# Layer 0's norms of pairs 2 to 4 applied to the rows as they lie, their mean and scale spread by DMA

## The chip, the cores and the metric

The kernel runs on one core of a Trainium2 chip. The metric is the device time of one launch in microseconds (us), the median of several runs. The engines are named as the profile names them: PE does matmuls and transposes, DVE is the vector engine, ACT the scalar engine, POOL is GpSimd, and SP issues most of the DMAs. Each engine works through its own queue in order.

## The reference

The input x is 8 batches of 512 tokens by 512 features. It passes through two blocks, and each adds its result to x.

```python
x = x + xcond(layernorm(x))   # 4 layers of a gated recurrence, in two directions, and a fusion
x = x + ffn(layernorm(x))     # ternary weights, 512 -> 2048 -> 512, gelu and a layernorm between

def stack(x):                 # once along the tokens, once against them, with the same weights
    h = x
    for i in range(4):
        z = sigmoid(h @ Wz[i].T + bz[i])
        a = clip(1 - z, 1e-8, 1 - 1e-8)
        g = tanh(h @ Wz[i].T + bz[i])          # the same matrix and bias serve both gates here
        h_new = scan(a, z * g)                 # s[t] = a[t] * s[t-1] + (z * g)[t]
        if i > 0:
            h_new = h_new + h
        h = layernorm(h_new) * gamma + beta    # over the 512 features of a token
    return h
```

The two directions' results are joined and multiplied by the fusion matrix. What matters here is the layernorm after layer 0: each token has a mean and a variance over its 512 features.

## The kernel before

**Layout.** The recurrence runs along the tokens, so the states lie with features on the partitions and tokens along the row: a state is four chunks of 128 features by 512 tokens. A layernorm wants the other layout. `norm` therefore does it in two moves. A *turn* (`turned`, `tokens`) takes one tile of 128 tokens: four PE transposes (L316) into the PSUM tile `pt`, of which there are two buffers; then on DVE `bn_stats` (L171), `bn_aggr` (L173), the variance with its epsilon (L177) and the negative mean (L182); on POOL the power -0.5 (L178); on ACT the normalise step (L188, L189) into a token tile. When all four token tiles stand, a *turn-back* (`back`) takes one chunk of features: four PE transposes (L325) into the PSUM tile `pf`, and on ACT the step with gamma and beta (L331) into the state `h`.

**Batches and pairs.** Batches are worked in pairs, (0,1), (2,3), (4,5), (6,7). A sequence `s` is (batch, direction). For one pair, layers 1 to 3 run over its four sequences in turn; each sequence of a layer is four steps of `gates`: eight matmul instructions (L487) for one chunk, three gate functions on ACT (L505 to L507), the clamp on POOL (L511), and on DVE the product (L514), the scan (L518) and the residual (L588). Then `fusion` of this pair (L622, L632; eight tiles of 128 tokens) is interleaved with `first_layer` of the next pair (L535). In layer 0 both directions share the matmul and the gates, and the two scans leave four chunks `zf` (forward) and four chunks `zb` (backward). Layer 0 works on raw x: its product is multiplied by the token's scale `scale[b]` (L546), which `scale_x` makes from four PE transposes of a column spread over 128 columns and one ACT copy (L385, L389).

**The order.** Everything is put in order by hand in `slot`. A slot does its main work, then what is due (`stages`, by name), then a share of the queues `turns` and `backs`, then the slot's scans, then the ACT steps of those shares; `now` counts slots. An entry of a queue is taken in order and only when it is ready: a turn from the slot that it was queued for, a turn-back one slot after its fourth token tile. A slot takes `cap` entries of each queue (2 beside a fusion tile, otherwise 1), and a second one if that entry is late by its `piece`. `pair` sets how many entries share one piece. `held` counts the token tiles in use (a pool of 10), `zlive` the chunks of z (a pool of 16). `need(s)` empties the queues of s before its next layer.

After layer 3, `norm_last` needs only each token's scale, not the mean; for sequences (3,0), (5,0) and (7,0) `by_scalar` measures it on ACT, in two passes with accumulation (`two_passes`, L396 to L398), and for all others DVE does it. During the changes of pairs, each fusion tile also takes up to three `pieces` of another job: weights of the second block are staged by DMA (L646), made ternary on DVE (L193, L194) and stored again (L679).

**The second block** starts when the recurrence is done and isn't touched.

Of the kernel before, what the change touches and what calls it, by code (L numbers as in the profile page):

```python
# [9 lines left out]
F32 = mybir.dt.float32  # L10
F32R = mybir.dt.float32r
AF = mybir.ActivationFunctionType
ALU = mybir.AluOpType
# [3 lines left out]
P = 128  # L17
LN_EPS = 1e-5
# [6 lines left out]
def kernel(  # L25
# [26 lines left out]
    nc = tc.nc  # L52
    B, S, H = x.shape
    L = gru_wT.shape[0]
    F = fc_wT.shape[1]
    NC_ = H // P
    NT = S // P
# [7 lines left out]
    small = ctx.enter_context(tc.tile_pool(name="small", bufs=8))  # L65
    wpool = ctx.enter_context(tc.tile_pool(name="wts", bufs=1))
    hp = ctx.enter_context(tc.tile_pool(name="h", bufs=6))
    dram = ctx.enter_context(tc.tile_pool(name="x1", bufs=1, space=bass.MemoryType.DRAM))

    tokp = ctx.enter_context(tc.tile_pool(name="tok", bufs=TOK))  # L70
    xsp = ctx.enter_context(tc.tile_pool(name="xs", bufs=12))
    zp = ctx.enter_context(tc.tile_pool(name="z", bufs=ZT))
    ps_f = ctx.enter_context(tc.tile_pool(name="ps_f", bufs=2, space=PSUM))
# [34 lines left out]
    gam = const.tile([P, NC_], F32, name="gam")  # L108
    bet = const.tile([P, NC_], F32, name="bet")
# [11 lines left out]
    for i in range(2):  # L121
# [3 lines left out]
        s = fusp.tile([P, P], F32R, name=f"fpick{i}")  # L125
# [36 lines left out]
    ident = const.tile([P, P], F32, name="ident")  # L162
    make_identity(nc, ident)
    mhalf = const.tile([P, 1], F32, name="mhalf")
# [64 lines left out]
    with rec:  # L229
        gp = rec.enter_context(tc.tile_pool(name="gate", bufs=3))  # L230
# [6 lines left out]
        now = [0]  # L237
        state = {}
        rsv = {}
        turns, backs = [], []  # L240

        held = [0]

        class Tokens(list):
# [4 lines left out]
            def append(self, tile_):  # L249
                super().append(tile_)  # L250
                self.at = now[0] + self.lag

        def ready(at):
            if isinstance(at, Tokens):
                return len(at) == NT and at.at <= now[0]
            return at <= now[0] and held[0] < TOK

        def shares(cap):


            last = []
            for q in (turns, backs):
                some = []
                for i in range(max(2, cap)):
                    if not q or not ready(q[0][0]):
                        break
                    at, piece = q[0][:2]
                    late = (at.at if isinstance(at, Tokens) else at) + piece <= now[0]
                    if i >= cap and not late:
                        break  # L270
                    some.append(take(q))
                last = some + last
            return last

        zlive = [0]
# [3 lines left out]
        def queue(q, key, at, piece, go):  # L279
            left[key] = left.get(key, 0) + 1  # L280
            q.append((at, piece, key, go))
# [27 lines left out]
        def turned(zs, t, name, frees=0):  # L309
            def source():  # L310
                if t == NT - 1:
                    zlive[0] -= frees
                spare = name.startswith("00_0") and t > 1
                pt = (ps_f if spare else ps_t).tile([P, H], F32, tag="pf" if spare else "pt", name=f"pt_{name}")
                for c in range(NC_):
                    nc.tensor.transpose(pt[:, ts(c, P)], zs[c][:, ts(t, P)], ident)  # L316
                return pt
            return source
# [21 lines left out]
        def norm(s, zs, tag, pause, pair=1):  # L340

            toks, at = Tokens(), now[0] + pause

            def dst():
                if s not in state:
                    state[s] = hp.tile([P, NC_, S], F32, tag="h", name=f"h_{s[0]}{s[1]}")
                return state[s]

            for t in range(NT):
                queue(turns, s, at, t // pair, tokens(turned(zs, t, f"{tag}_{t}", NC_), toks, None, f"{tag}_{t}"))  # L350
            for c in range(NC_):
                queue(backs, s, toks, c // pair, back(toks, dst, c, True, f"{tag}_{c}"))

        def norm_last(s, tag):
            rsv[s] = small.tile([P, NT], F32, tag="rsv", name=f"rsv_{tag}")
            zs = [state[s][:, c, :] for c in range(NC_)]
            for t in range(NT):
                source, name = turned(zs, t, f"{tag}_{t}"), f"{tag}_{t}"
                queue(turns, s, now[0] + NC_ + 1, t, by_scalar(s, t, source, name) if s[0] > 1 and s[0] % 2 and s[1] == 0 else
                      tokens(source, None, rsv[s][:, t : t + 1], name))  # L360

        def by_scalar(s, t, source, name):

            def go():
                src = source()
                left[s] += 1

                def last():
                    end = two_passes(src, src, rsv[s][:, t : t + 1], name)

                    def rest():
                        end()
                        left[s] -= 1
                    stages.append((now[0] + 1, "late", rest))
                return last
            return go

        rx, scale = {}, {}

        def scale_x(b):  # L380

            def go():
                pf = ps_f.tile([P, S], F32, tag="pf", name=f"pr_{b}")
                for t in range(NT):
                    nc.tensor.transpose(pf[:, ts(t, P)], rx[b][:, t : t + 1].broadcast_to([P, P]), ident)  # L385

                def last():
                    scale[b] = gp.tile([P, S], F32, tag="scale", bufs=2, name=f"scale_{b}")
                    nc.scalar.copy(scale[b], pf)  # L389
                return last  # L390
            return go
# [56 lines left out]
        stages = []  # L448
# [64 lines left out]
        def product(z, t):  # L513
            nc.vector.tensor_tensor(z, z, t, ALU.mult)  # L514
# [7 lines left out]
        def first_layer(b, lag=0):  # L522


            zf, zb = [], []

            def chunk(o):
                def work():
                    while zlive[0] + 2 > ZT:
                        slot(None, 2)  # L530
                    zlive[0] += 2
                    name = f"{b}_0_{o}"
                    u = ps_u.tile([P, S], F32, tag="u", name=f"u_{name}")
                    for c in range(NC_):
                        nc.tensor.matmul(  # L535
                            u, lhsT=gw[0][:, c, ts(o, P)], rhs=xT[b][:, c, :],
                            start=(c == 0), stop=(c == NC_ - 1),
                        )
                        if (b, o, c) in midway:
                            midway.pop((b, o, c))()  # L540

                    wait = 1 if (b, o) == (0, 0) else 0

                    def scaled():
                        z = zp.tile([P, S], F32, tag="z", name=f"z_{name}")
                        nc.vector.tensor_tensor(z, u, scale[b], ALU.mult)  # L546
                        a, t = factors(z, z, 0, o, name)

                        stages.append((now[0], "clamps", lambda: clamp(nc.gpsimd, a)))
                        if wait:  # L550
                            for i, v in enumerate((bet, gam)):
                                nc.vector.tensor_copy(both[:, :, i, :], v.unsqueeze(2).broadcast_to([P, NC_, 64]))

                        def scans():
                            product(z, t)
                            f = zp.tile([P, S], F32, tag="z", name=f"zf_{name}")
                            scan(f, a, z, False)
                            zf.append(f)
                            if o == NC_ - 1:
                                state[b, 0] = xT.pop(b)  # L560
                                norm((b, 0), zf, f"{b}0_0", 2 if b == 1 else 1, 2 if b < 2 else 1)

                            def backward():
                                scan(z, a, z, True)
                                zb.append(z)
                                if o == NC_ - 1:
                                    norm((b, 1), zb, f"{b}1_0", 2 if b == 1 else 1, 2 if b < 2 else 1)
                            if b == 0:
                                stages.append((now[0] + 1, "resid", backward))
                            else:  # L570
                                backward()
                        stages.append((now[0] + 1 - wait, "scans", scans))
                    stages.append((now[0] + lag + wait, "factors", scaled))
                return work
            return [chunk(o) for o in range(NC_)]
# [295 lines left out]
    for i in range(2):  # L871
# [5 lines left out]
        s = const.tile([P, P], F32R, name=f"pick{i}")  # L877
# [137 lines left out]
    for j in range(ends):  # L1015
        b, k = divmod(j, NF)
        late = []
# [22 lines left out]
        at = 12 if b == 0 else 8  # L1040
# [57 lines left out]
```

## Time and profile before

| | |
|---|---|
| median of 3 runs | 1713.0 us (1712.42 to 1713.18) |
| the profiled execution | 1712.95 us, its span 1711.2 us |
| busy in the span | PE 1700.3, DVE 1389.1, ACT 1089.5, POOL 377.2 us |
| granted TensorE clock | 1.00 throughout |
| recurrent part | the last fusion begins at 1158.9 us |
| changes of pairs | 263.9 to 358, 561.9 to 656, 859.6 to 953 us |

An execution's time is longer than its span by what lies around the first and the last instruction. The page's groups give for each line its engine, the tile written and the tiles read, the shape, the count, the busy time and mean length of one, and the engine's idle time just ahead of it. Matmul lengths overlap one another, so a group's busy time divided by its count is the share of one. Busy times of engines may all be high at once, since they work beside each other; what sets the time is in the chain.

### The profile page before, as it was taken

How to read it: one execution, taken by the hardware profiler on the slowest of the kernel's cores; microseconds unless marked ns; L12 is line 12 of the kernel's file. 1: busy time of each engine (PE TensorE's matmuls, PEld its weight loads, DVE VectorE, ACT ScalarE, POOL GpSimd, SP SyncE). 2: the span in 40 equal slices, each digit the busy share in tenths (PEclk: the TensorE clock that was granted, in tenths of full speed). 3: DMA queues.
4: the chain of work that ended last, by engine and by line, in shares of the span. 5: the costliest groups of instructions: out<-in, count | busy, mean ns of one | idle time of the engine just before them, and what ended most of it. 6: DMA issues, size and time to landing. Idle time of an engine off the chain costs nothing.

```text
span 1711.2 us, 19776 instructions
## 1 busy us (share of the span) xinstructions
PE 1700.3 (99%) x6440; PEld 1042.6 (61%) x6440; DVE 1389.1 (81%) x2619; ACT 1089.5 (64%) x1918; POOL 377.2 (22%) x558
## 2 busy tenths in 40 slices
PE   9999999999999999999999999999999999999999
PEld 5455554555555455555545555554688888888887
DVE  7988889889887888888788888885568768768877
ACT  5898873468886346888535688862356566666654
POOL 3333333223332222333222222321000000000000
PEclk9999999999999999999999999999999999999999
DMA  7002231150000125000012200102201101100100
GB/s 271 19 25 81 98 93 37 66 193 19 13 1 1 56 68 191 19 13 1 1 56 75 98 28 22 75 1 99 74 1 50 50 1 50 50 21 30 50 19 31
DMA packets 46599, 91.75 MB, mean 54 GB/s; under 512 B 5280, under 2 KB 5536, under 8 KB 45472
## 3 DMA queue, kind: packets, MB, share of 16 engines
q1 hardware_dynamic: 45488, 88.78, 15.1%
q10 hardware_dynamic: 1008, 1.70, 0.3%
q8 instruction: 51, 0.84, 0.2%
q14 instruction: 52, 0.43, 0.1%
HBM read 65.30 MB, written 25.17 MB: 53 GB/s over the span
## 4 chain that ended last, share of the span: by engine, by line
PE 92%; DVE 5%; ACT 2%; POOL 1%; issue 0%; DVEq 0%
PE u L487 33%; PE po L937 14%; PE ph L910 14%; PE pu L622 13%; PE u L535 6%; PE pt L316 6%; PE pf L325 4%; DVE z L518 1%; PE py L214 1%; DVE z L514 1%; DVE st L171 1%; ACT tok L189 1%; DVE z L588 1%; PE pst L948 0%; POOL rs L178 0%
## 5 line engine op out<-in xcount | busy, mean ns | idle before, releaser
L487 PE MATMUL u<-xT,gw 128*128 128x512 f32 x768 | 345.5, 593 | 0.0
L487 PE MATMUL u<-h,gw 128*128 128x512 f32 x768 | 345.5, 592 | 0.0
L518 DVE TENSOR_TENSOR_SCAN z<-a,z 128x512 f32<-128x512 f32 x224 | 277.1, 1237 | 21.8 <-DVE z L514 0.9
L511 POOL TENSOR_SCALAR a<-a 128x512 f32<-128x512 f32 x224 | 150.3, 671 | 559.2 <-ACT a L505 558.3
L487 PEld LDWEIGHTS u<-xT,gw 128*128 128x128 f32 x768 | 138.6, 190 | 138.7 <-issue 137.0
L487 PEld LDWEIGHTS u<-h,gw 128*128 128x128 f32 x768 | 138.6, 190 | 138.2 <-issue 138.2
L505 ACT ACTIVATE a<-u,ngb 128x512 f32<-128x512 f32 x192 | 131.7, 686 | 142.4 <-PE u L487 140.9
L937 PE MATMUL po<-pwq,ghi 128*128 128x512 f32 x512 | 202.8, 396 | 0.0
L171 DVE BATCH_NORM_STATS2 st<-pt 128x6 f32<-128x512 f32 x244 | 169.3, 694 | 39.2 <-PE pt L316 32.5
L937 PE MATMUL po<-pwq,glo 128*128 128x512 f32 x512 | 199.7, 390 | 0.0
L910 PE MATMUL ph<-yhi,fcq 128*128 128x512 f32 x512 | 199.7, 390 | 0.0
L910 PE MATMUL ph<-ylo,fcq 128*128 128x512 f32 x512 | 199.4, 389 | 0.0
L514 DVE TENSOR_TENSOR z<-z,t 128x512 f32<-128x512 f32 x224 | 154.8, 691 | 52.6 <-ACT z L507 52.3
L914 ACT ACTIVATE g<-ph 128x512 f32<-128x512 f32 x128 | 76.4, 597 | 186.6 <-PE ph L910 186.6
L178 POOL TENSOR_TENSOR rs<-ve,mhalf 128x1 f32<-128x1 f32 x192 | 125.5, 654 | 155.1 <-DVE nmu L182 152.7
L189 ACT ACTIVATE tok<-pt,nmr,rs 128x512 f32<-128x512 f32 x192 | 149.4, 778 | 6.4
L925 DVE TENSOR_TENSOR acc<-acc,g 128x512 f32<-128x512 f32 x112 | 77.4, 691 | 85.0 <-ACT g L914 84.1
L507 ACT ACTIVATE z<-u,gb 128x512 f32<-128x512 f32 x192 | 132.4, 690 | 0.0
L506 ACT ACTIVATE t<-u,gb 128x512 f32<-128x512 f32 x192 | 130.8, 681 | 0.0
L316 PEld LDWEIGHTS pt<-ident,z 128*128 128x128 f32 x640 | 78.7, 141 | 77.2 <-issue 48.9
L535 PE MATMUL u<-xT,gw 128*128 128x512 f32 x256 | 114.8, 593 | 0.8 <-DVE gw L767 0.8
L622 PE MATMUL pu<-fw,xT 128*128 128x512 f32 x256 | 115.2, 593 | 0.0
(164 smaller groups left out, 2621.0 us busy)
## 6 DMA issues: line engine op xcount, KB each, us to landing
xf<-in_x_dram SPq DMA_DIRECT2D x32, 256.0 KB, 5.5
x<-xf SPq DMA_DIRECT2D x32, 256.0 KB, 2.0
xy<-x SPq DMA_DIRECT2D x32, 256.0 KB, 4.0
xn<-in_x_dram SPq DMA_DIRECT2D x31, 256.0 KB, 4.5
out_dram<-xy SPq DMA_DIRECT2D x31, 256.0 KB, 2.0
xT<-in_xt_dram SPq DMA_DIRECT2D x7, 1024.0 KB, 7.7
fca<-in_fc_wT_dram SPq DMA_DIRECT2D x16, 256.0 KB, 2.9
pwa<-in_proj_wT_dram SPq DMA_DIRECT2D x16, 256.0 KB, 2.6
```

What stands on the lines that cost most here:

```text
L171: nc.vector.bn_stats(st, src)
L189: nc.scalar.activation(dst, src, AF.Identity, bias=nmr, scale=rs)
L316: nc.tensor.transpose(pt[:, ts(c, P)], zs[c][:, ts(t, P)], ident)
L487: nc.tensor.matmul(u, lhsT=gw[l][:, c, ts(o, P)], rhs=h[:, c, :], start=(c == 0), stop=(c == NC_ - 1),)
L507: nc.scalar.activation(z, u, AF.Sigmoid, bias=gb[:, l, o : o + 1])
L511: engine.tensor_scalar(a, a, CLAMP_HI, CLAMP_LO, ALU.min, ALU.max)
L514: nc.vector.tensor_tensor(z, z, t, ALU.mult)
L518: nc.vector.tensor_tensor_scan(dst[:, d], a[:, d], z[:, d], 0.0, ALU.mult, ALU.add)
L535: nc.tensor.matmul(u, lhsT=gw[0][:, c, ts(o, P)], rhs=xT[b][:, c, :], start=(c == 0), stop=(c == NC_ - 1),)
L622: nc.tensor.matmul(pu, lhsT=hs[d][:, c, ts(t, P)], rhs=fw[:, d * NC_ + c, :], start=(c == 0), stop=(c == NC_ - 1),)
L910: nc.tensor.matmul(ph, lhsT=w, rhs=ys[b][c][i], start=(c == 0 and i == 0), stop=(c == NC_ - 1 and i == 1),)
L937: nc.tensor.matmul(po[b][t], lhsT=part[:, ts(t, P)], rhs=pwq[k // NP_][:, k % NP_, :], start=(k == 0 and i == 0), stop=(k == NF - 1 and i ...
```

## The change

For batches 2 to 7, layer 0's two norms no longer turn the tokens back. The chunks `zf` and `zb` stay as they lie. Each token's mean and scale are found from the turned tiles (turns 0 and 1 by ACT in two passes with accumulation, turns 2 and 3 by DVE's `bn_stats`) and gathered in one tile `pk` of 128 x 2 x 4. One POOL instruction makes the four scales. `to_rows` then turns `pk` with one PE transpose, copies the eight rows to SBUF on ACT, stores them as two rows of 512 in DRAM, and loads each row spread over all 128 partitions into a tile of the token pool. `apply` subtracts the one and multiplies by the other on DVE, chunk by chunk, in place; ACT applies gamma and beta as before. Such a chunk is ready three slots after the rows were sent (`LANDS`). Batches 0 and 1 keep the old way.

The token scale of x of batches 2 to 7 goes the same way: one transpose, one ACT copy, a store and one spread load in place of four transposes and a copy. Last, `by_scalar` now also serves (2,0), (4,0) and (6,0), and the norms of layer 0 of batches 3, 5 and 7 are queued in pieces of two.

```diff
+        class Rows:
+            at = None
         def ready(at):
+            if isinstance(at, Rows):
+                return at.at is not None and at.at <= now[0]
...
+        LANDS = 3
+        def to_rows(cols, n, dsts, tag):
+            turned_ = ps_f.tile([P, S], F32, tag="pf", name=f"prow_{tag}")[0 : n * NT, 0:P]
+            nc.tensor.transpose(turned_, cols.rearrange("p i t -> p (i t)"), ident)
+            short = dsts[0][0 : n * NT, 0:P]
+            nc.scalar.copy(short, turned_)
+            row = dram.tile([n, S], F32, tag=f"row_{tag}", name=f"row_{tag}")
+            nc.sync.dma_start(out=row.rearrange("i (t p) -> (i t) p", p=P), in_=short)
+            for i, dst in enumerate(dsts):
+                nc.sync.dma_start(out=dst, in_=row[i : i + 1, :].broadcast_to([P, S]))
+
+        def norm_rows(s, zs, tag, pause, pair=1):
+            rows_, at = Rows(), now[0] + pause
+            pk = small.tile([P, 2, NT], F32, tag="pk", bufs=6, name=f"pk_{tag}")
+            wide = []
+            def close():
+                nc.vector.tensor_scalar(pk[:, 1, :], pk[:, 1, :], LN_EPS, None, ALU.add)
+                nc.gpsimd.tensor_tensor(pk[:, 1, :], pk[:, 1, :], mhalf.broadcast_to([P, NT]), ALU.pow)
+                stages.append((now[0] + 1, "late", send))
+            def send():
+                for i in range(2):
+                    wide.append(tokp.tile([P, S], F32, tag="tok", name=f"wide{i}_{tag}"))
+                to_rows(pk, 2, wide, tag)
+                rows_.at = now[0] + LANDS
+            def turn(t):
+                source, name = turned(zs, t, f"{tag}_{t}"), f"{tag}_{t}"
+                def go():
+                    src = source()
+                    if t == 0:
+                        held[0] += 2
+                    if t >= 2:
+                        st = small.tile([P, 6], F32, tag="st", name=f"st_{name}")
+                        nc.vector.bn_stats(st, src)
+                        nc.vector.bn_aggr(pk[:, :, t], st)
+                        if t == NT - 1:
+                            close()
+                        return lambda: None
+                    def last():
+                        sm, ss = (small.tile([P, 1], F32, tag=k, name=f"{k}_{name}") for k in ("sm", "ss"))
+                        mean, var = pk[:, 0, t : t + 1], pk[:, 1, t : t + 1]
+                        nc.scalar.activation(src, src, AF.Copy, accum_out=sm)
+                        nc.scalar.activation(mean, sm, AF.Copy, scale=1.0 / H)
+                        nc.scalar.activation(src, src, AF.Square, bias=mean, scale=-1.0, accum_out=ss)
+                        nc.scalar.activation(var, ss, AF.Copy, scale=1.0 / H)
+                    return last
+                return go
+            def apply(c):
+                def go():
+                    nc.vector.tensor_tensor(zs[c], zs[c], wide[0], ALU.subtract)
+                    nc.vector.tensor_tensor(zs[c], zs[c], wide[1], ALU.mult)
+                    zlive[0] -= 1
+                    if c == NC_ - 1:
+                        held[0] -= 2
+                    def last():
+                        if s not in state:
+                            state[s] = hp.tile([P, NC_, S], F32, tag="h", name=f"h_{s[0]}{s[1]}")
+                        nc.scalar.activation(
+                            state[s][:, c, :], zs[c], AF.Identity,
+                            bias=bet[:, c : c + 1], scale=gam[:, c : c + 1],
+                        )
+                    return last
+                return go
+            for t in range(NT):
+                queue(turns, s, at, t // pair, turn(t))
+            for c in range(NC_):
+                queue(backs, s, rows_, c // pair, apply(c))
...
-                queue(turns, s, now[0] + NC_ + 1, t, by_scalar(s, t, source, name) if s[0] > 1 and s[0] % 2 and s[1] == 0 else
+                queue(turns, s, now[0] + NC_ + 1, t, by_scalar(s, t, source, name) if s[0] > 1 and s[1] == 0 else
...
+            def spread_x():
+                scale[b] = gp.tile([P, S], F32, tag="scale", bufs=2, name=f"scale_{b}")
+                to_rows(rx[b].unsqueeze(1), 1, [scale[b]], f"x{b}")
+            if b > 1:
+                return spread_x
...
-                                norm((b, 0), zf, f"{b}0_0", 2 if b == 1 else 1, 2 if b < 2 else 1)
+                                (norm if b < 2 else norm_rows)((b, 0), zf, f"{b}0_0", 2 if b == 1 else 1, 2 if b < 2 or b % 2 else 1)
...
-                                    norm((b, 1), zb, f"{b}1_0", 2 if b == 1 else 1, 2 if b < 2 else 1)
+                                    (norm if b < 2 else norm_rows)((b, 1), zb, f"{b}1_0", 2 if b == 1 else 1, 2 if b < 2 or b % 2 else 1)
```

More of the change, by code (lines that the diff above doesn't have):

```diff
@@ L267, in shares @@
                     at, piece = q[0][:2]
-                    late = (at.at if isinstance(at, Tokens) else at) + piece <= now[0]
+                    late = (at.at if isinstance(at, (Tokens, Rows)) else at) + piece <= now[0]
                     if i >= cap and not late:
```

## Prediction, made before the change was run

> **What bounds the kernel now.** I read the page's busy line and slices first, then the chain, then the groups that the change touches, and last the stretches around one change of pairs.
>
> ```profile
> PE 1700.3 (99%) x6440; PEld 1042.6 (61%) x6440; DVE 1389.1 (81%) x2619; ACT 1089.5 (64%) x1918; POOL 377.2 (22%) x558
> ...
> PE   9999999999999999999999999999999999999999
> ...
> DVE  7988889889887888888788888885568768768877
> ...
> PE 92%; DVE 5%; ACT 2%; POOL 1%; issue 0%; DVEq 0%
> ```
>
> PE is never free and holds 92% of the chain: whatever leaves PE shortens the run, as long as no other engine makes PE wait. But DVE stands at 80 to 90% in the recurrent part (slices 1 to 28): it is the next bound, and it has about a tenth to give. These groups carry the edit:
>
> ```profile
> L514 DVE TENSOR_TENSOR z<-z,t 128x512 f32<-128x512 f32 x224 | 154.8, 691 | 52.6 <-ACT z L507 52.3
> ...
> L171 DVE BATCH_NORM_STATS2 st<-pt 128x6 f32<-128x512 f32 x244 | 169.3, 694 | 39.2 <-PE pt L316 32.5
> ...
> L325 PE MATMUL pf<-ident,tok 128*128 128x128 f32 x768 | 112.4, 273 | 1.2 <-ACT tok L189 1.0 <-ACT h L331 0.2
> ```
>
> Now the stretches round the second change of pairs, from batches 2, 3 to 4, 5 (columns: window, length, busy PE, PEld, DVE, ACT, POOL). I number its slots from 0, the first fusion tile; slots 0 to 15 are the fusion tiles and layer-0 chunks, and slot 16 is the first of layer 1.
>
> ```profile
> 580.00:600.00 20.00, 20.00 (x60) 9.70 (x59) 19.24 (x32) 3.62 (x8) 4.16 (x6) 1.00 0.24 79
> 627.20:639.70 12.50, 12.50 (x46) 6.66 (x45) 10.62 (x24) 6.81 (x12) 2.73 (x4) 1.00 0.40 122
> 639.70:655.60 15.90, 15.90 (x54) 8.15 (x53) 12.43 (x19) 4.84 (x7) 0.61 (x1) 1.00 0.52 176
> 655.60:673.50 17.90, 17.51 (x67) 9.43 (x66) 15.63 (x40) 14.73 (x27) 6.58 (x10) 1.00 0.80 277
> 673.50:691.20 17.70, 17.70 (x71) 9.85 (x70) 14.59 (x29) 14.38 (x26) 4.97 (x8) 1.00 0.14 47
> ```
>
> Slots 12 to 23 take 627.2 to 691.2: 64.0 us, PE full but for 0.39, DVE busy 53.3. The first row is the fullest that DVE gets anywhere: 96%.
>
> **PE.** A group of four transposes holds PE 0.4375 us (the chain: "0.87 PE pf L325 x8"), so 0.109 each; the row's mean of 273 ns is overlapped length. Twelve norms (6 batches, 2 directions) lose 16 turn-backs and gain one transpose: 12 x 15 = 180. Six x scales go from 4 transposes to 1: 18. Together 198 x 0.109 = **21.7 us off PE**, of which 6 x 3 x 0.109 = 2.0 are the x scales and 6.6 fall in each of the three changes of pairs. The Trainium skill ("TensorE: Matmul & The Clock Gate", Part 4) gives some 275 ns for a 128x128 transpose inside a kernel. By it the saving would be an estimated 54 us, and the rows' pitch contradicts it.
>
> **DVE, the price.** Each norm gains a subtract and a multiply over four chunks. A dependent pair runs as L514 before a scan does: 0.79 to the dependent start and 0.61 to the next, 1.4 us, so 5.6 a norm. It loses two of four stats (a whole group has a pitch of 1.07: 0.73 + 0.22 + 0.07 + 0.05) to ACT, and in the other two the 0.13 of variance and shift.
>
> When this lands is read from the code. A norm's turns come when its scans are done; the row is sent one slot after the last turn; the chunks are taken from three slots later. So (4,0): turns in slots 8 to 10, sent 11, chunks in 14 and 15. (4,1): turns 10 to 12, sent 13, one chunk in each of 16 to 19. (5,0): turns 15, 16, sent 17, chunks in 20, 21. (5,1): turns 17, 18, sent 19, chunks in 22, 23. All sixteen pairs fall into slots 14 to 23, close before layer 1 reads what they make, and twelve of them into slots whose PE part has just become shorter (an undisturbed gates slot with one turn and one turn-back was 4.31; now 3.44 to 4.42).
>
> DVE in slots 12 to 23: 53.3 + 16 x 1.4 = 75.7, less four whole groups (4.3) and small ones (0.3): 71.1. PE alone would need 64.0 - 0.4 - 6.3 = 57.3. **DVE now has more to do than the stretch lasted.** With DVE never idle it is 71.1 - 64.0 = 7.1 longer, and 0.3 is saved in slot 11: +6.8 a change of pairs, the floor. At 96%, its fullest row, 71.1/0.96 = 74.0: +9.8.
>
> PE cannot run ahead of DVE there: it needs chunk 3 of h(4,1) at slot 20, made in slot 19 behind all of slot 18's scans; h(5,0) at 24 from slot 21; and the turns of layer 1 at 21 need slot 19's residual. The lag of a slot with 6.5 of DVE against 3.9 of PE is passed on, and in the run after it PE is full again, so it isn't won back.
>
> **ACT.** Turns 0 and 1 of each norm are measured by ACT. Two such turns in the profile of before, in ACT's own order of time:
>
> ```profile
> 569.36 0.58 ACT L396 ACTIVATE pt<-pt 128x512 f32<-128x512 f32 x1 [5.90 <-PE pt L316]
> ...
> 570.99 0.59 ACT L396 ACTIVATE pt<-pt 128x512 f32<-128x512 f32 x1
> ```
>
> One takes 1.63, and the new one has a further small copy (L397, 0.20): 1.85. In slots 15 and 17 two stand together, 3.7, behind the affine steps (0.67 each) and ahead of the next slot's three gate functions (1.75). Slot 17 asks 1.75 + 0.2 + 0.67 + 3.7 = 6.3 of ACT against 4.4 of PE. They also hold both pt buffers, so PE's turns of slots 16 and 18 wait for them. I walked the three queues slot by slot with these pitches, on the clock of before. PE unhindered would begin slot 16 at 652.4. DVE makes (4,0)'s last chunk at 656.1, behind three ternary pieces (3.6), ACT its affine step at 656.9 and the two turns until 660.5; so PE's slot 17 begins at 660.9, 4.2 late. ACT's turns of slot 17 end at 672.0, and slot 19 begins 7.0 late; slot 21, behind (4,1)'s last chunk, 8.4. Slots 24 and 25 wait for DVE's stats (slots 21 to 23 hold 6.5 of DVE each) and the tokens behind them, and slot 26 begins at 710.2, against 699.3 in the profile of before: 10.8. The x stats in slot 21 (1.0), the third ternary's load in slot 15 (0.9) and 0.1 at each hand-over bring it to 13.8. I keep that as the upper end, since every queue order in it has to be right, and 9.8 as the value. What ACT loses (four normalise steps at 1.07) lies earlier or beside this.
>
> **POOL.** One power of 128x4 (1.02, L956) takes the place of four (0.65): nothing. But the clamp L511 is 614 ns in the median and 1594 at most, and DVE's L616 took 1.08 and L194 1.04 where they met a clamp, against 0.68 and 0.75. The Trainium skill ("SBUF — State Buffer", SBUF: two separate sides) calls the port pair of the two engines an exclusive lock for a whole instruction when DVE has two SBUF inputs; the new steps have that. By the rows a meeting costs DVE 0.3 to 0.4. Eight of the gates slots hold new steps: 0 to 3.0 a change of pairs; I take 1.5.
>
> **DMA and SP's queue.** Each norm adds a 4 KB store and two spreads of 256 KB; each x scale a store and one spread. By the rows a store lands in 2.0 (x<-xf) and a load in 4.0 to 4.5 (xy, xn): about 7 with the issues. From send to use PE has 15, 18, 11.6 and 10.9 us, so it is covered; uncovered it would be up to 7 each. SP waits at each store for ACT's copy, and behind it stand the staged ternary loads (L646), the stores of x1 (L635) and the loads of xn. The third ternary of slot 15 waited 1.55 for its load already. The others are wanted much later. The x scales were copied at 546.98 and 555.16, and the first fusion tile alone, ahead of the first layer-0 chunk, runs from 561.85: covered by the 6.7 us between and that tile (6.9): nothing.
>
> **Last norm by ACT for even batches.** 12 turns move 1.03 each off DVE onto ACT (1.63), in slots where ACT idles 2.03 before each gate (541 to 562). Nothing, and some 0.3 a turn if that cover were gone.
>
> **Sum.** Per change of pairs: 9.8 + 1.5 = 11.3, PE's saving there already inside. Three of them +33.9, x scales -2.0: +31.9. The profiled execution took 1712.95 (span 1711.2 and 1.75 around it), the median is 1713.0: **1745**. The ends: floor 3 x 6.8 - 2.0 = +18.4, 1731; walk with meetings 3 x 16.8 - 2.0 = +48.4, 1761.
>
> **The rivals.** *PE's saving comes through.* DVE's slack is taken up and PE stays full: 1712.95 - 21.7 = 1691. For it speaks PE's 99%; against it that DVE would have to do 71.1 us of work in 57. It decides if DVE's new steps spread over 71.1/0.96 = 74 us of PE time or more, that is some four slots more than I give them, without PE needing them: 0.09. *A draw.* Part of the lag is hidden by work of the next layer: within 3.4 us of before, 0.04. *The round trip is late too.* In the window of slots 15 to 17 the xf loads took 9.5 to land: with that, (5,0) and (5,1) come up to 2.7 late. As PE waits for the same chunks it adds 2 x 2.7 x 3 = 16: 1761, 0.10. *It doesn't do what it says:* each back queue is served in order, so none of the 16 turn-backs can stay; no weight of its own.
>
> **The numbers.** My forecast holds 0.77. A measurement of this kernel can tell about 0.2%, 3.4 us, from no change. Faster 0.09, same 0.04, slower 0.87. Below 1718 lie the rival of PE, the draw and a little of the slower cases, 0.15; above 1762 some 0.05. The slower cases' own range is 1728 to 1762.
>
> **What would show it.** Right: pf<-ident,tok falls from 768 to 576; new DVE groups of 48 subtracts and 48 multiplies at 0.69; in the 50 us after slot 14 of each change DVE at 95% or more, PE's digit under 9 there, and PE waits for DVE's stats, ACT's passes and h; elsewhere as before. DVE's busy sum rises by 96 x 0.69 - 24 x 0.88 - 48 x 0.3 + 2 - 12 x 0.88, about 22. Wrong: PE at 99% still and slots 14 to 23 no longer than the 51.5 us of before (639.7 to 691.2); or waits of DVE on the spread tiles, which would make DMA the cause.

## The result, and the profile after

The change makes the kernel slower: a median of 1757.4 us against 1712.8, a ratio of 1.0261 (95% interval 1.0243 to 1.0279), 44.6 us more. The forecast was 1745, with a range of 1718 to 1762. The profiled execution took 1758.03, its span 1756.0. One of the four executions of one kernel below (all stats on DVE) took 3579.0 us and is left out of its time.

The page's busy line, the slices of PE, DVE and the granted clock, and the chain by engine:

```profile
PE 1702.9 (97%) x6242; PEld 1025.8 (58%) x6242; DVE 1416.8 (81%) x2559; ACT 1104.8 (63%) x2038; POOL 366.8 (21%) x522
...
PE   9999999988999998799999889999999999999999
...
DVE  8988888889887888898688898876468778768777
...
PEclk9999999989999999999999999999999999999999
...
PE 81%; DVE 13%; ACT 3%; issue 1%; DMA 1%; POOL 1%; DVEq 0%; ACTq 0%
```

PE has 198 transposes fewer, and yet it is busy for longer: 1702.9 us against 1700.3. It also idles 53.1 us of the span (1756.0 - 1702.9) where it idled 10.9. Its digit falls below 9 in three places, the slices after each change of pairs, and nowhere else. DVE has gone from 5% to 13% of the chain.

The groups after (the same columns as before):

```profile
L581 PE MATMUL u<-xT,gw 128*128 128x512 f32 x768 | 363.1, 617 | 8.1 <-ACT xT L429 8.1
...
L332 PE MATMUL pf<-ident,tok 128*128 128x128 f32 x576 | 86.9, 274 | 8.9 <-ACT tok L189 8.7 <-ACT h L338 0.2
...
L421 DVE TENSOR_TENSOR zf<-zf,wide 128x512 f32<-128x512 f32 x24 | 17.5, 728 | 0.8
...
L420 DVE TENSOR_TENSOR z<-z,wide 128x512 f32<-128x512 f32 x24 | 16.4, 682 | 0.0
```

The turn-backs have gone from 768 to 576, as they should. DVE's new steps last 0.68 to 0.73 us in the mean, and DVE never idled ahead of the subtracts (0.0; the forward group's row says the same): the spread rows were always there in time. The recurrence's matmuls over the forward direction's states (they lie in `xT`) hold PE 363.1 us for the same 768 instructions that took 345.5: a slower clock, not more work.

Round the second change of pairs, the stretches of slots 12 to 15, 16 to 19, 20 to 23, and then slots 24, 25 and most of 26 (window, length, busy PE, PEld, DVE, ACT, POOL, granted clock, the DMA engines' busy share, GB/s):

```profile
642.37:667.83 25.46, 25.46 (x72) 11.87 (x71) 23.32 (x35) 7.81 (x16) 2.25 (x3) 1.00 0.55 163
667.83:694.23 26.40, 20.70 (x60) 9.46 (x59) 20.66 (x33) 16.64 (x39) 4.47 (x5) 0.87 0.34 113
694.23:710.96 16.73, 15.54 (x47) 7.10 (x46) 15.48 (x26) 11.02 (x19) 4.75 (x5) 1.00 0.70 251
710.96:735.00 24.04, 15.40 (x43) 7.01 (x42) 21.64 (x41) 14.55 (x26) 7.02 (x9) 0.86 0.13 44
```

Slots 12 to 15 are shorter by what PE lost: 25.46 against 28.41 (627.23 to 655.64). Slots 20 to 23 are 0.94 shorter (16.73 against 17.67). That is all the gain there is in these stretches. Slots 16 to 19 take 26.40 against 17.85, and the last stretch 24.04, not quite to the end of slot 26, against 12.5 for the whole of the same three slots. From the start of slot 12 to the start of slot 26 it is 86.4 (642.37 to 728.75) against 72.1.

What PE waits for there, in PE's order of time:

```profile
672.34 3.48 PE L581 MATMUL u<-xT,gw 128*128 128x512 f32 x4 [2.63 <-ACT xT L429]
...
687.05 0.66 PE L323 MATMUL pt<-ident,z 128*128 128x128 f32 x4 [1.49 <-ACT pt L412]
...
718.07 0.66 PE L323 MATMUL pt<-ident,z 128*128 128x128 f32 x4 [3.52 <-ACT tok L189]
...
724.46 0.55 PE L323 MATMUL pt<-ident,z 128*128 128x128 f32 x3 [2.29 <-ACT tok L189]
...
728.48 0.48 PE L332 MATMUL pf<-ident,tok 128*128 128x128 f32 x1 [2.56 <-ACT tok L189]
```

The first is slot 16 waiting for the affine step of a chunk that DVE made late; the second is slot 18 waiting for a PSUM tile that ACT is still measuring; the last three are slots 24 and 25, where a token tile is late. The releaser named is ACT, but the chain shows who made ACT late. In order of time (start, length):

```profile
705.91 0.61 DVE zf L420
706.54 0.69 DVE zf L421
707.23 0.61 DVE zf L420
707.87 0.69 DVE zf L421
708.56 0.61 DVE st_x L171
...
709.57 0.61 DVE z L608
710.27 1.24 DVE z L612
711.53 0.92 DVE z L682
712.45 0.62 DVE st L171
```

DVE works without a wait through its work of slots 20 to 24: two chunks' steps, x's stats, the product, the scan and the residual, and only then the stats that a waiting turn needs.

### The profile page after: what moved, and what is told of

Read it like the earlier page. It is cut to its first block, busy times and chain, and to the rows that moved or that the text cites. A ratio compares the mean times of both kernels' runs of the same rounds, so it can differ in the third digit from the quotient of the medians.

```text
span 1756.0 us, 19487 instructions
## 1 busy us (share of the span) xinstructions
PE 1702.9 (97%) x6242; PEld 1025.8 (58%) x6242; DVE 1416.8 (81%) x2559; ACT 1104.8 (63%) x2038; POOL 366.8 (21%) x522
## 3 DMA queue, kind: packets, MB, share of 16 engines
q1 hardware_dynamic: 50048, 96.71, 16.3%
## 4 chain that ended last, share of the span: by engine, by line
PE 81%; DVE 13%; ACT 3%; issue 1%; DMA 1%; POOL 1%; DVEq 0%; ACTq 0%
PE u L581 28%; PE po L1031 13%; PE ph L1004 13%; PE pu L716 10%; PE u L629 6%; PE pt L323 5%; PE pf L332 3%; DVE z L612 3%; DVE z L608 2%; DVE z L682 1%; DVE st L171 1%; DVE zf L421 1%; DVE z L421 1%; PE py L214 1%; DVE zf L420 1%
## 5 line engine op out<-in xcount | busy, mean ns | idle before, releaser
L581 PE MATMUL u<-xT,gw 128*128 128x512 f32 x768 | 363.1, 617 | 8.1 <-ACT xT L429 8.1
L581 PEld LDWEIGHTS u<-xT,gw 128*128 128x128 f32 x768 | 144.3, 198 | 157.3 <-issue 142.6
L171 DVE BATCH_NORM_STATS2 st<-pt 128x6 f32<-128x512 f32 x184 | 127.7, 694 | 29.9 <-PE pt L323 22.9
L323 PE MATMUL pt<-ident,z 128*128 128x128 f32 x640 | 96.1, 275 | 22.7 <-ACT tok L189 16.2
L629 PE MATMUL u<-xT,gw 128*128 128x512 f32 x256 | 115.0, 593 | 1.1 <-DVE gw L861 0.8
L716 PE MATMUL pu<-fw,h 128*128 128x512 f32 x256 | 115.1, 592 | 0.0
```

The lines of the kernel that those rows point to most:

```text
L171: nc.vector.bn_stats(st, src)
L581: nc.tensor.matmul(u, lhsT=gw[l][:, c, ts(o, P)], rhs=h[:, c, :], start=(c == 0), stop=(c == NC_ - 1),)
L629: nc.tensor.matmul(u, lhsT=gw[0][:, c, ts(o, P)], rhs=xT[b][:, c, :], start=(c == 0), stop=(c == NC_ - 1),)
L716: nc.tensor.matmul(pu, lhsT=hs[d][:, c, ts(t, P)], rhs=fw[:, d * NC_ + c, :], start=(c == 0), stop=(c == NC_ - 1),)
```

## The experiments

Theory A is that of the prediction: DVE's queue, with ACT's two-pass turns, holds PE in slots 14 to 25. Theory B is the round trip of the rows. A third question came from the profile: what the slower clock costs. Each time stands beside runs of the kernel of before on the same chip, 1712.6 to 1712.7.

**The x scales alone.** The last norms and layer 0's norms are as before.

```diff
-(norm if b < 2 else norm_rows)((b, 0), zf, f"{b}0_0", 2 if b == 1 else 1, 2 if b < 2 or b % 2 else 1)
+norm((b, 0), zf, f"{b}0_0", 2 if b == 1 else 1, 2 if b < 2 else 1)
-(norm if b < 2 else norm_rows)((b, 1), zb, f"{b}1_0", 2 if b == 1 else 1, 2 if b < 2 or b % 2 else 1)
+norm((b, 1), zb, f"{b}1_0", 2 if b == 1 else 1, 2 if b < 2 else 1)
-by_scalar(s, t, source, name) if s[0] > 1 and s[1] == 0 else
+by_scalar(s, t, source, name) if s[0] > 1 and s[0] % 2 and s[1] == 0 else
```

> Only the x scales go through the row and its spread; layer 0's norms and the last norms are as before. Theory A (PE is the bound, and the extra DMAs are covered): 18 transposes of 0.109 us leave PE, 1712.8 - 2.0 = 1710.8, and PE stays full. Theory B (the round trip is waited for): the first layer-0 chunk of a pair waits for its scale, and the time is at or above 1713.

1710.9 against 1712.6, a ratio of 0.9991 (0.9982 to 0.9999). PE's busy time falls from 1700.3 to 1698.0. This small part of the change does about what PE's count says (1.7 us of the 2.0).

**DVE's steps left out.**

```diff
-                    nc.vector.tensor_tensor(zs[c], zs[c], wide[0], ALU.subtract)
-                    nc.vector.tensor_tensor(zs[c], zs[c], wide[1], ALU.mult)
```

> The change without DVE's 96 subtract and multiply steps: the rows are still measured, sent and spread, but not applied, so layer 0's states are left unnormalised. Theory A (DVE's queue, with ACT's two-pass turns, holds PE): DVE has 71.1 - 22.4 = 48.7 us to do in slots 12 to 23 against 57.3 of PE, and PE's saving comes through, less the waits for ACT's turns in slots 16 and 18 (0 to 3 us a change of pairs): 1691 to 1701, granted clock 1.00. If ACT's turns were the main cause, the time would stay above 1730. It doesn't tell the round trip apart, as nothing waits for the rows here.

1696.2, a ratio of 0.9904 (0.9890 to 0.9917). Its busy line:

```profile
PE 1680.8 (99%) x6242; PEld 1020.3 (60%) x6242; DVE 1351.5 (80%) x2463; ACT 1100.5 (65%) x2038; POOL 367.0 (22%) x522
```

The same PE, ACT and DMA instructions as the change, the clock at 1.00, and 61 us faster. So the 96 steps, 65 us of DVE's busy time (1416.8 - 1351.5), cost 61 us of the kernel's. It also parts the change's loss cleanly, span against span: 1756.0 - 1694.0 = 62.0, of which 39.9 are PE's idle time (53.1 - 13.2) and 22.1 are PE's busy time (1702.9 - 1680.8), the same instructions at a lower clock.

**The steps kept, the wait for the rows taken away.**

```diff
-                    nc.vector.tensor_tensor(zs[c], zs[c], wide[0], ALU.subtract)
-                    nc.vector.tensor_tensor(zs[c], zs[c], wide[1], ALU.mult)
+                    nc.vector.tensor_tensor(zs[c], zs[c], scale[s[0]], ALU.subtract)
+                    nc.vector.tensor_tensor(zs[c], zs[c], scale[s[0]], ALU.mult)
```

> The change with both DVE steps of every chunk as they are, but reading the batch's x scale, which has long lain in SBUF, in place of the two spread rows; the rows are still sent and spread, and the normalisation is wrong by that. Theory A (DVE's work): nothing changes, 1757 within 3. Theory B (PE and DVE wait for the round trip): the waits go, and it falls to 1745 or below.

1757.5, a ratio of 1.0263 (1.0249 to 1.0277) where the change has 1.0261. Theory B falls: nothing waits for the trip through DRAM. `LANDS` is still 3 in this run, so the chunks are taken in the same slots; what it costs that the trip puts DVE's steps three slots behind the send was not tested by itself.

**Half the length.** Both steps over the first 256 tokens.

```diff
+                    nc.vector.tensor_tensor(zs[c][:, 0 : S // 2], zs[c][:, 0 : S // 2], wide[0][:, 0 : S // 2], ALU.subtract)
+                    nc.vector.tensor_tensor(zs[c][:, 0 : S // 2], zs[c][:, 0 : S // 2], wide[1][:, 0 : S // 2], ALU.mult)
```

> The change with the subtract and the multiply over the first 256 of 512 tokens only (the other half stays unnormalised). Theory A: DVE's added work falls from 22.4 to about 12 us a change of pairs; its 61 us stand against 57 of PE, so most of the loss goes: 1700 to 1722. If the number of steps or the hand-over counted and not their length, it would stay above 1745.

1733.2, a ratio of 1.0119 (1.0103 to 1.0134): between the two expectations, and so a miss for theory A's number. The half-width steps are more than half as long (lines of the group: duration in ns, least, median and most):

```profile
L420 DVE TENSOR_TENSOR zf<-zf,wide x24: 398/416/419, 346.4 to 999.3; 128x256 f32<-128x256 f32 x24
```

At 0.42 against 0.69 they leave three fifths of the added work, and three fifths of the loss remain (37.0 of 61.3 us above the kernel without them). The loss goes with DVE's added time. My 1700 to 1722 took DVE's sum against PE's sum over the whole stretch, as if one could fill the other's gaps.

**All stats on DVE.**

```diff
-                    if t >= 2:
+                    if t >= 0:
```

> The change with all four turns of each norm measured by DVE's bn_stats, none by ACT. If ACT's two-pass turns (two together in slots 15 and 17) are what carries the walk from 9.8 to 13.8 us a change of pairs, the waits of slots 16 and 18 for pt go and the time falls by up to 12: 1745, less what DVE's 4 more groups in slots 12 to 23 (0.95 each, 3.8) give back, 11 us: 1746 to 1757. If DVE's queue alone is the bound, the 3.8 come on top: 1765 to 1770.

1762.6, a ratio of 1.0292 (1.0275 to 1.0309), 5 us above the change and between the expectations. DVE's 11.4 us more (3 x 3.8) cost only some 5; by this difference ACT's two-pass turns are worth about 6 us, 2 a change of pairs. It is a difference of two terms that I didn't measure apart. In the change itself PE's waits for a tile that ACT is measuring come to 3.1 us in all (three waits for L412), so by both numbers ACT's turns are a small part of the loss.

**The subtract on POOL.**

```diff
-                    nc.vector.tensor_tensor(zs[c], zs[c], wide[0], ALU.subtract)
+                    nc.gpsimd.tensor_tensor(zs[c], zs[c], wide[0], ALU.subtract)
```

> The change with the subtract on POOL and only the multiply on DVE. By DVE's work alone this is like the half-width steps: about 1733. But a two-input step on POOL may be longer than DVE's 0.69, its clamps stand behind it, and the two engines' two-input steps may block one another: if they do, 1745 or above, with longer multiplies or clamps in the groups.

1796.6, a ratio of 1.0484 (1.0467 to 1.0502): 39 us worse than the change. POOL's step and DVE's multiply (ns, least, median, most):

```profile
L420 POOL TENSOR_TENSOR zf<-zf,wide x24: 1262/1358/1713, 342.0 to 1055.5; 128x512 f32<-128x512 f32 x24
```

```profile
L421 DVE TENSOR_TENSOR z<-z,wide x24: 677/692/1736, 370.8 to 1072.9; 128x512 f32<-128x512 f32 x24
```

The step is twice as long on POOL, DVE's multiply must wait for it in DVE's queue (46 us in 24 waits, over both directions), and some multiplies grow to 1.74. The work left DVE, but DVE's queue stood still for it.

**The ternary pieces earlier.**

```diff
-                    pieces((1, 2, 1, 0, 1, 2, 2, 3)[t + (b % 2) * NT])
+                    pieces((3, 2, 2, 1, 1, 1, 1, 1)[t + (b % 2) * NT])
```

> The change with the same twelve ternary pieces a change of pairs taken earlier: 3, 2, 2, 1 beside the first batch's fusion tiles and 1 each beside the second's, so slots 14 and 15 hold two in place of five. Theory A: 3.6 us less of DVE ahead of slot 16 and no wait for a staged load there; slot 16's wait for the last chunk (2.4 to 3.1) and part of ACT's lateness behind it go: 3 to 5 a change of pairs, 1742 to 1748. If only the slots of layer 1 count, no change: 1757.

1743.2, a ratio of 1.0176 (1.0160 to 1.0191): 14 us back, 4.7 a change of pairs. The wait in slot 16 for a chunk is gone; those of slots 18, 24 and 25 stand as they were (1.49, 3.52, 2.29 and 2.56).

**Idle matmuls in PE's gaps.**

```diff
+        def fill(n):
+            if n:
+                dump = ps_u.tile([P, S], F32, tag="u", name=f"dump_{now[0]}")
+                for _ in range(n):
+                    nc.tensor.matmul(dump, lhsT=gw[1][:, 0, 0:P], rhs=gw[1][:, 1, :], start=True, stop=True)
```

> The change with idle matmuls (128x512, 0.86 us each, read by nobody) put into PE's gaps: 3 ahead of slot 16, 2 at the end of slot 18, 4 of slot 24, 2 of slot 25 and 3 ahead of the next turn-back, 42 in all, 36 us of PE. If PE's clock, which reads 0.50 for some us after a wait of 2.3 to 3.5, costs time on the chain, the granted clock returns to 1.00 and the time falls, though PE is given more to do: by 8 to 15, 1742 to 1749. If the slow stretches lie beside DVE's queue and cost nothing, 1757 or above.

1752.9, a ratio of 1.0234 (1.0219 to 1.0250), against 1.0261 for the change: 4.5 us faster with 38.5 us more of PE work (84 instructions). Without the fills PE is busy for 1723.5 - 38.5 = 1685.0, close to the 1680.8 of the kernel without DVE's steps, and the granted clock is 0.998. So nearly all of the slow clock went, and only 4.5 us of the time with it: it lies between what I expected of a clock on the chain (1742 to 1749) and beside it (1757 or more). By that, most of the 22 us of slower matmuls lay beside DVE's queue. The 4.5 is not a clean price of the clock: the two ratios' intervals overlap a little (one ends at 1.0250, the other begins at 1.0243), and the fills may themselves delay a turn here and there, so the clock's share may be larger.

**The last norms of even batches by DVE again.**

```diff
-by_scalar(s, t, source, name) if s[0] > 1 and s[1] == 0 else
+by_scalar(s, t, source, name) if s[0] > 1 and s[0] % 2 and s[1] == 0 else
```

> The change with the last norms of (2,0), (4,0) and (6,0) measured by DVE again, as before. The prediction costed that move at nothing, as ACT idles 2.0 us ahead of each gate there: 1757 within 2. If that move loads ACT where it matters, it is faster by up to 10; if it frees DVE where DVE is short, slower by up to 12.

1757.8, a ratio of 1.0261 (1.0247 to 1.0275). That part of the change costs and gives nothing.

**One norm of four, where DVE has room.** Only the forward norm of batches 2, 4 and 6, two slots after the send, with the pieces earlier and the x scales spread.

```diff
-(norm if b < 2 else norm_rows)((b, 0), zf, f"{b}0_0", 2 if b == 1 else 1, 2 if b < 2 or b % 2 else 1)
+(norm if b < 2 or b % 2 else norm_rows)((b, 0), zf, f"{b}0_0", 2 if b == 1 else 1, 2 if b < 2 else 1)
-(norm if b < 2 else norm_rows)((b, 1), zb, f"{b}1_0", 2 if b == 1 else 1, 2 if b < 2 or b % 2 else 1)
+norm((b, 1), zb, f"{b}1_0", 2 if b == 1 else 1, 2 if b < 2 else 1)
-        LANDS = 3
+        LANDS = 2
-                queue(backs, s, rows_, c // pair, apply(c))
+                queue(backs, s, rows_, c // 2, apply(c))
-                    pieces((1, 2, 1, 0, 1, 2, 2, 3)[t + (b % 2) * NT])
+                    pieces((3, 2, 2, 1, 1, 1, 1, 1)[t + (b % 2) * NT])
```

(The last norms are as in the kernel of before.)

> Only the forward norm of the first batch of each pair (2, 4, 6) goes to the rows, with its chunks two slots after the send, in slots 13 and 14; the other three norms turn back as before; the x scales are spread; the ternary pieces are taken earlier (3, 2, 2, 1 and 1, 1, 1, 1); last norms as before. Theory A: DVE gains 5.6 us a change of pairs in slots that have that much to spare (29 of DVE against 30.5 of PE in slots 12 to 16), so PE's 15 x 0.109 us come through: 1712.6 - 2.0 - 4.9 = 1705.7, 1704 to 1709. If any application on DVE costs more than it saves, it stays above 1711.

**1705.0**, a ratio of 0.9954 (0.9940 to 0.9968): faster than both kernels, and 0.7 from the number worked out. Its busy line:

```profile
PE 1692.9 (99%) x6377; PEld 1035.7 (61%) x6377; DVE 1398.6 (82%) x2610; ACT 1085.8 (64%) x1933; POOL 370.9 (22%) x549
```

PE is busy for 7.4 us less than before (the count gave 6.9), and idles 10.2 of the span of 1703.1 where it idled 10.9. So the gain is work that has left PE. The run changes several things at once; only the pieces (next run) and the x scales (first run) are told apart, `LANDS` 2 is not.

**The same with the pieces where they were.**

```diff
-                    pieces((3, 2, 2, 1, 1, 1, 1, 1)[t + (b % 2) * NT])
+                    pieces((1, 2, 1, 0, 1, 2, 2, 3)[t + (b % 2) * NT])
```

> The same with the ternary pieces where they were (1, 2, 1, 0 and 1, 2, 2, 3). Theory A: slots 12 to 16 then hold 3.6 us more of DVE, about 33 against 30.5 of PE; the pieces of slot 15 no longer stand ahead of a chunk that layer 1 waits for, so 0 to 2 us a change of pairs are lost again: 1705 to 1711.

1723.2, a ratio of 1.0060 (1.0047 to 1.0072): 18 us above the last one and outside what I expected. The work of each engine is the same in both; only the slots of the twelve ternary pieces of a change of pairs differ: eight or four of them beside the first batch's fusion tiles, two or five in slots 14 and 15. The stretch 660 to 670 us of the two, the earlier pieces first (the columns as above):

```profile
660.00:670.00 10.00, 9.84 (x38) 5.31 (x37) 9.27 (x23) 8.81 (x17) 4.71 (x7) 1.00 1.01 366
```

```profile
660.00:670.00 10.00, 5.93 (x19) 3.48 (x18) 8.01 (x19) 6.14 (x11) 2.27 (x4) 0.83 0.62 196
```

And the chain of the second through its gap, in order of time:

```profile
657.34 0.76 DVE pwq L194
658.12 2.49 DMA wq_pw<-pwq
...
661.24 0.75 DVE pwq L194
661.99 0.62 DVE st L171
...
664.00 0.79 ACT tok L189
...
664.83 0.73 PE pt L323 x4
```

I had looked at the chunks alone. But DVE is behind. It begins slot 15's first piece 0.3 us before PE begins slot 16 (656.83 and 657.16); in the kernel before it was 7.5 ahead (648.19 and 655.64). At the third piece it idles for another 1.43, ending at 660.71: finished pieces lie in two buffers (`qp`, bufs=2), and the first piece's store, issued at 658.12, takes 2.49 to land and free its buffer. The stats of two turns stand behind that piece; the token behind those stats holds `pt`, and PE's next turn waits 4.07 for it. The clock is 0.83 over that stretch.

## Why the prediction was right, and where its sizes were off

**PE's saving.** 21.7 us were worked out. PE's busy time falls by 19.5 in the kernel without DVE's steps (1700.3 - 1680.8), and by 2.3 for the x scales alone against 2.0. That is 0.098 and 0.128 a transpose, so the pitch of 0.109 holds as a price. The 275 ns of the Trainium skill ("TensorE: Matmul & The Clock Gate", Part 4) agree with the rows' mean length of 273, and not with what a transpose costs in these runs.

**DVE's price, the main term: right.** The slots were as read from the code (the sends of (4,0), (4,1), (5,0) and (5,1) lie in slots 11, 13, 17 and 19 of the trace, the chunks in 14 to 23). Without the steps the loss is gone, with half their length it is three fifths, and with one norm's steps where DVE has room PE's saving comes through.

**The size: mis-sized in the choice between two estimates.** I had a sum of DVE's work over the fullest rate seen (9.8 a change of pairs) and a walk of the three queues (13.8), and took the sum. From the first fusion tile of one change of pairs to that of the next, or of the last fusion, it now takes 16.3, 15.6 and 14.0 longer (314.2, 313.4 and 313.3 against 298.0, 297.8 and 299.3), the x scales' saving inside. The sum went wrong in two ways. It took DVE to be 96% busy, and DVE is busy for 59.5 of the 68.6 us of slots 12 to 23, 87%; in the 50 us from slot 14 it is 85%, where I had named 95% as a sign of being right. DVE itself waits there: 2.01 for a turn of PE at the end of slot 16. And the sum looked at slots 12 to 23 alone: round the second change they became 4.7 longer (68.6 against 63.9), while slots 24 and 25 became 9.6 longer (17.8 against 8.2), as PE came to the steps that DVE still had in its queue.

The walk had slots 24 and 25 in it. It put slot 17 4.2 late, slot 19 7.0, slot 21 8.4 and slot 26 10.8 before its last three terms; the trace has PE reach slot 17 5.4 late (677.54 against 672.14 unhindered), slot 19 8.1 and slot 26 14.3 after the same slot 12. With 13.8 the sum is 3 x 13.8 - 2.0 = +39.4, 1752.3; with the 1.5 for POOL's clamps as well it is 3 x 15.3 - 2.0 = +43.9, 1756.9, against 1757.4. That close a hit would have been partly luck, since the walk is early in each of its slots and has no term for the clock. The half-width run shows the same fault of such sums: an engine's spare time can't be spent where the queue doesn't stand.

**A wait with the wrong reason.** I wrote that the third ternary piece of slot 15 waits for its load. The rows name a store, `wq_pw<-pwq`, before and after:

```profile
652.19 0.49 DVE L193 TENSOR_SCALAR pwq<-pwb,lo_pw 128x512 f32<-128x512 f32 x1 [1.55 <-DMA wq_pw<-pwq]
```

```profile
668.84 0.49 DVE L193 TENSOR_SCALAR pwq<-pwb,lo_pw 128x512 f32<-128x512 f32 x1 [1.28 <-DMA wq_pw<-pwq]
```

It is the store that frees one of the two buffers. In the change it lies ahead of the chunk that slot 16 waits for. The wait goes with the place of three pieces in a row: with one norm and the pieces earlier, DVE waits 1.27 at the third piece of slot 0 (567.11) and not in slot 15.

**The clock: left out.** I had no term for it, although the waits that the walk gave were 2 to 4 us long. It reads 0.50 for some microseconds after several of them. By the fills it is worth some 4.5 us of the time, near what a measurement can tell; how much it is in truth stays open.

**Meeting POOL's clamps.** I took 1.5 a change of pairs. The multiplies average 728 and 709 ns over 24 each where 692 is undisturbed, 1.3 us in all three changes, and in the chain residuals of 0.91 to 0.95 against 0.69 stand in slots 16, 20 and 21. The residuals average 708 and 709 over 64 each where they were 692, 2.1 us more in all. Together that is some 1 a change of pairs: right in kind, a little too high. The run with POOL's subtract shows the same meeting at its worst, a multiply of 1.74.

**DMA and SP's queue, last norms by ACT, x scales.** All three were costed at nothing or at their PE count, and the runs with the wait taken away (1757.5), with DVE's last norms (1757.8) and with the scales alone (1710.9) bear that out. For SP's queue it holds but for the store above.

**The rivals.** PE's saving didn't come through because its condition, DVE's steps spread over some four slots more, isn't met. With one norm of four the steps fall where DVE has room, and the saving comes through. The round trip had no part as a wait; by `LANDS` it still says in which slots DVE's steps fall, and no run moves that alone.

## What to carry to other kernels

When PE is full and another engine stands at 80 to 90% beside it, price work moved onto that engine slot by slot, in queue order, and on past the last slot that holds new work: the sum over a stretch was low here by a third (9.8 against some 15 a change of pairs). Look for the few results that PE will wait for next, and for what stands ahead of them in the queue; taking the unrelated ternary pieces earlier was worth 18 us with one norm, where the best kernel gains 7.7 in all, and 14 us with four. A move that is a loss for all four norms can be a gain for the one whose steps fall where the other engine has room.

## What the runs showed of the hardware that I had not expected

The granted clock halves inside a kernel whose PE is busy for 97% of the span. Windows of 3 us in the change (window, length, busy PE, PEld, DVE, ACT, POOL, granted clock):

```profile
669.00:672.00 3.00, 0.71 (x2) 0.00 (x0) 2.93 (x5) 0.53 (x1) 0.00 (x0) 0.99 0.78 286
672.00:675.00 3.00, 2.66 (x3) 1.12 (x4) 2.14 (x4) 2.42 (x6) 0.00 (x0) 0.50 0.00 0
...
715.00:718.00 3.00, 0.00 (x0) 0.00 (x0) 2.86 (x4) 2.45 (x5) 0.00 (x0) 1.00 0.00 0
718.00:721.00 3.00, 2.93 (x10) 1.64 (x11) 2.86 (x8) 1.75 (x4) 1.59 (x2) 1.00 0.00 0
```

A wait of 2.63 was followed by a clock of 0.50, and one of 3.52 was not. In the first change of pairs PE waits 3.52 at the same place, and there the clock is 0.50 from 406 to 409 us:

```profile
405.44 0.88 PE L323 MATMUL pt<-ident,z 128*128 128x128 f32 x4 [3.52 <-ACT tok L189]
```

So the length of a wait doesn't decide alone. The Trainium skill ("TensorE: Matmul & The Clock Gate", Part 1) describes a free-running window of about 3.4 us, and a halved clock after an idle window. Two waits of 3.52 that end differently would fit, if one filled a window and the other fell across two; the wait of 2.63 is shorter than such a window, and the rule as stated doesn't cover it. Where the windows lay is not in the trace, and no run here shows it.

A two-input step on POOL took 1.26 us at least against 0.69 on DVE for 128x512, and both engines' steps reached 1.7 where they met.
